# A cross-attention block with a recurrent mixer: set-up inside the score buffers, first loads in order of need, exponentials and late loads held at set places

## The chip, the cores and the metric

The kernel runs on one core of a Trainium2 chip. Its engines are TensorE (PE: matrix products and transposes), VectorE (DVE), ScalarE (ACT), GpSimd (POOL) and the sync engine (SP), which here issues the DMA transfers. Each engine works through its own list of instructions in order. The metric is the time of one execution on the device in microseconds (us); the median of the runs is compared. All numbers are float32.

## The reference

Three layers follow one another on x, 32 batches of 64 rows of 256:

```python
x = x + xattn(layernorm(x), ctx_768, w_q, w_kv, w_out, b_out)
x = x + attn(layernorm(x), time_decay, time_first, time_mix_*, Wk, Wv, Wr, Wo, bo)
x = x + ffn(layernorm(x), w1, b1, w2, b2)
```

The first is cross-attention with 16 heads of 64 over 1601 context rows of 192 per batch: q from x, k and v from the context, softmax over the keys, a projection back to 256. The second mixes each row with the one before it, makes k, v and r with Wk, Wv, Wr, runs a decaying sum over the 64 rows (decay exp(-exp(time_decay))), divides, gates by a sigmoid and projects with Wo. The third is two matrix products with a relu between them.

## The kernel before, in words

Keys are never formed. The key weights are folded into the queries instead: for each head, q times the transposed key weights gives a vector of 192 that is multiplied with the context rows themselves. The 192 are held as 128 ("lo") and 64 ("hi").

**Set-up.** The key half of w_kv (`wk_lo`, `wk_hi`) is transposed by TensorE into `wkT` (L304, L305, evicted at L308). Then `queries(tg)` runs for four groups `tg` of eight batches (512 rows of x). It normalises four tiles of x (statistics L110, L111, `xn` L177), transposes them (`xnT`, L185, L188), and for four head groups `g` of four heads each makes q (`q_ps`, L195, evicted as `qT` by ScalarE, L202), the folded lo part (`ql_ps`, L211, evicted as `q_lo` half by VectorE L218 and half by ScalarE L219) and the hi part (`qh_ps`, L226, evicted as `q_hi` by VectorE, L233, L234). Each head group is stored to a DRAM tensor `q_dram` (L236, L242). `q_lo` and `q_hi` have two buffers each, so the group after next waits for the store to have landed. PSUM holds six banks for the folded parts and two for all else. `q_load(b)` brings one batch's folded queries back (L163). `blocks_load(b)` loads the context of a batch in blocks of 32 columns (`cb`, twelve transfers, L153), and `ctx_prep(b)` turns these on VectorE into the transposed context `cT` (stream transposes L260, L261), with two small transfers (L255, L262).

**Late weights.** The weights wanted only later (`wv_lo`, `wv_hi`, `wo_sb`, the four square matrices `nat_*`, biases and per-channel columns) are loaded in set-up, after the first block loads, on the sync queue. At the end of set-up TensorE transposes the square matrices into `rw_T` (L320, evicted by VectorE L325); `td_rows`, rows of the decay, are made from two exponentials (L328 to L331).

**Attention.** The main loop goes over 64 half-batches `u`: a batch `b` and eight of its heads. `scores` makes for 1601 keys the products of `cT` and q: six blocks of twelve products of 512 columns (L475) and a rest (L494). ScalarE copies each block from PSUM to `s_sb` (L482, L501); there are two PSUM buffers for blocks and two buffers of `s_sb`. VectorE keeps a running maximum `m2` (L484, L486), then `mx` (L504, L505); GpSimd reduces it over partitions into `mb` (L512). Four parts follow, each a subtraction on VectorE (L522) and an exponential on ScalarE (L523). While the scores of half `u` run, the previous half's exponentials are summed on VectorE (`t2`, `sum`, L547 to L551), reduced by GpSimd (`den`, L555) and inverted (L565 to L569); its weighted sums `o_lo` (L344, called from `av_lo`) and `o_hi` (L592, L602) come after the scores, and VectorE scales them into `oT` (L618). The loop is a software pipeline: at `u == 1` the parts of half 0 are given to `scores` as hooks, called after blocks 2, 3, 4 and 5; later halves do their parts after `av_lo`. `fill` places pieces of the older tiles' work (projections, mixer) between the products of `av_lo`. The feed-forward layer closes the program.

**What sets the order.** A planner orders each engine's list at build time, by the program's order, priorities and modelled readiness; it may move an instruction forward where it thinks the operands are ready. On the chip each list is then fixed. A tile of a pool shares memory with earlier tiles that were released: set-up's pool is closed before the pool `attn` (scores, maxima) opens, so the first uses of `attn` wait for the last readers and transfers of what lay there.

Of the kernel before, what the change touches and what calls it, by code (L numbers as in the profile page):

```python
# [15 lines left out]
P = 128  # L16
# [4 lines left out]
def kernel(  # L21
# [69 lines left out]
    nc.sync.dma_start(x_sb[:, 0:4, :], xr[:, 0:4, :])  # L91
# [25 lines left out]
    with ExitStack() as st_b:  # L117
        with ExitStack() as st_a:
            kp = st_a.enter_context(tc.tile_pool(name="keys", bufs=2))
            cpool = st_a.enter_context(tc.tile_pool(name="ctx", bufs=1))  # L120
            aw = st_a.enter_context(tc.tile_pool(name="aw", bufs=1))
            wv_lo = aw.tile([P, INNER], F32, name="wv_lo")
            wv_hi = aw.tile([P, INNER], F32, name="wv_hi")
            wo_sb = aw.tile([P, INNER // P, D], F32, name="wo_sb")
# [44 lines left out]
            def queries(tg, sp, sps, wq_sb, wkT):  # L169

                TG = QB * T
                NX = TG // P
# [8 lines left out]
                xnT = sp.tile([P, 2, TG], F32, tag="xnT", name=f"xnT_{tg}")  # L181
                for c in range(2):
# [5 lines left out]
                    nc.vector.tensor_copy(xnT[:, c, :], pt)  # L188
                for g in range(NP // 2):
                    qT = sp.tile([P, 2, TG], F32, tag="qT", name=f"qT_{tg}_{g}", bufs=6)  # L190
                    for k in range(2):
                        hp = 2 * g + k
                        pq = sps.tile([P, TG], F32, tag="ps", name=f"q_ps_{tg}_{hp}")
                        for c in range(2):
                            nc.tensor.matmul(  # L195
                                pq,
                                lhsT=wq_sb[:, c, hp * P : (hp + 1) * P],
                                rhs=xnT[:, c, :],
                                start=(c == 0),
                                stop=(c == 1),  # L200
                            )
                        nc.scalar.activation(qT[:, k, :], pq, AF.Copy, scale=HD**-0.5)  # L202
                    lo = sp.tile([P, QB, 4, T], F32, tag="q_lo", name=f"q_lo_{tg}_{g}", bufs=2)
                    hi = sp.tile([P, QB, 2, T], F32, tag="q_hi", name=f"q_hi_{tg}_{g}", bufs=2)
                    for k in range(2):
                        pl = [
                            sps.tile([P, QB, T], F32, tag="f", name=f"ql_ps_{tg}_{g}_{k}_{o}", bufs=6)
                            for o in range(2)
                        ]
                        for o in range(2):  # L210
# [648 lines left out]
```

## Time and profile before

| | us |
|---|---|
| median of 3 runs | 2618.55 (2616.88 to 2618.9) |
| the profiled execution's own time | 2618.07 |
| its span | 2616.2 |
| TensorE busy in the span | 2588.2 |
| VectorE busy | 1908.3 |
| ScalarE busy | 953.6 |
| GpSimd busy | 356.4 |
| DMA, share of 16 engines (main queue) | 33.1% |

A profile row gives a start or a total, a duration, the engine and line, what is written and read, sizes and count; in brackets stands how long the engine was idle before it and what released it. A matrix product of float32 is shown as two instructions. Products are pipelined and their ends are modelled, so a busy TensorE may still be slowed by what it waits for. The granted clock of TensorE is 1.00 at full speed; the mean over this execution is 0.997.

### The profile page before, as it was taken

The page shows a single profiled execution, that of the slowest core. Times are in us where ns is not written, and L with a number is a line of the kernel's source. Part 1 is how long each engine was busy: PE and PEld are TensorE (multiplying, and loading weights), DVE is VectorE, ACT ScalarE, POOL GpSimd, SP SyncE. Part 2 cuts the span into 40 slices and gives each one's busy share as a digit, 9 for nine tenths or more (in the row PEclk, how much of TensorE's full clock was granted, in tenths as well). Part 3 has the DMA queues.
Part 4 walks back from the last instruction along what each step waited for, and adds up shares of the span by engine and source line. Part 5 has one row for each costly group of instructions (what it writes and reads, how often), then busy time and mean ns, then how long its engine had stood idle before and what let it go on. Part 6 is the DMA issues. An engine that isn't in the chain of part 4 may idle for free.

```text
span 2616.2 us, 33242 instructions
## 1 busy us (share of the span) xinstructions
PE 2588.2 (99%) x13824; PEld 1129.4 (43%) x13824; DVE 1908.3 (73%) x2283; ACT 953.6 (36%) x1019; POOL 356.4 (14%) x176
## 2 busy tenths in 40 slices
PE   8989999999999999999999999999999999999999
PEld 3333344444444444444444444444344444444466
DVE  4468878777786878777787868777787868787741
ACT  2233334333333334343433333343433434343221
POOL 0001111111111111111111111111111111111100
PEclk9989999999999999999999999999999999999999
DMA  8983333333322323233331323333331323310100
GB/s 201 273 174 54 58 56 63 45 63 63 63 57 50 60 42 63 45 63 63 63 63 44 63 39 63 49 59 63 63 63 44 63 49 54 63 26 20 52 11 22
DMA packets 437799, 169.63 MB, mean 65 GB/s; under 512 B 332400, under 2 KB 423952, under 8 KB 437648
## 3 DMA queue, kind: packets, MB, share of 16 engines
q1 hardware_dynamic: 437104, 166.46, 33.1%
q8 instruction: 108, 1.77, 0.3%
q10 hardware_dynamic: 544, 1.05, 0.1%
q14 instruction: 43, 0.35, 0.1%
HBM read 138.60 MB, written 27.26 MB: 63 GB/s over the span
## 4 chain that ended last, share of the span: by engine, by line
PE 95%; DMA 2%; DVE 1%; SPq 1%; issue 0%; POOL 0%; ACT 0%; DVEq 0%; POOLq 0%; ACTq 0%
PE s_ps L475 38%; PE o_lo L344 28%; PE o_hi L592 13%; PE s_ps_r L494 3%; PE fy L784 2%; PE v_ps L638 2%; PE h_ps L770 2%; PE y_ps L344 2%; PE q_ps L195 1%; DMA q_dram<-q_lo 1%; PE o_hi L602 1%; PE Wk_ps L344 1%; PE Wr_ps L344 1%; PE Wv_ps L344 1%; PE ry L344 1%; SPq L242 0%
## 5 line engine op out<-in xcount | busy, mean ns | idle before, releaser
L475 PE MATMUL s_ps<-q,cT 64*128 64x512 f32 x4608 | 1010.3, 594 | 8.0 <-ACT s_sb L482 7.1
L344 PE MATMUL o_lo<-s_sb,c 128*64 128x512 f32 (+1 forms) x3328 | 741.6, 594 | 0.0
L482 ACT COPY s_sb<-s_ps 128x1024 f32<-128x1024 f32 x384 | 388.7, 1012 | 955.6 <-PE s_ps L475 944.2
L475 PEld LDWEIGHTS s_ps<-q,cT 64*128 64x128 f32 x4608 | 442.2, 188 | 547.6 <-issue 537.9
L523 ACT ACTIVATE s_sb<-s_sb 128x2048 f32<-128x2048 f32 (+1 forms) x256 | 398.7, 1586 | 460.7 <-DVE s_sb L522 460.7
L522 DVE TENSOR_TENSOR s_sb<-s_sb,mb 128x2048 f32<-128x2048 f32 (+1 forms) x256 | 470.4, 1886 | 101.9 <-POOL mb L512 101.9
L486 DVE TENSOR_TENSOR m<-m,s_sb 128x1024 f32<-128x1024 f32 x256 | 313.6, 1225 | 169.6 <-ACT s_sb L482 157.7
L344 PEld LDWEIGHTS o_lo<-s_sb,c 128*64 128x64 f32 (+1 forms) x3328 | 231.1, 137 | 427.4 <-issue 417.7
L592 PE MATMUL o_hi<-s_sb,c 128*64 128x512 f32 x1536 | 340.4, 592 | 0.0
L555 POOL PARTITION_ALL_REDUCE den<-sum x64 | 207.4, 3241 | 834.1 <-DVE oT L618 666.3
L549 DVE TENSOR_TENSOR t<-t,s_sb 128x1024 f32<-128x1024 f32 x256 | 310.7, 1214 | 4.4
L512 POOL PARTITION_ALL_REDUCE mb<-mx x64 | 114.2, 1785 | 897.7 <-DVE mx L505 897.7
L565 DVE STREAM_TRANSPOSE turned<-den 128x512 f32<-128x512 f32 x64 | 45.5, 711 | 222.1 <-POOL den L555 222.1
L592 PEld LDWEIGHTS o_hi<-s_sb,c 128*64 128x64 f32 x1536 | 109.3, 136 | 211.3 <-issue 206.1
L494 PE MATMUL s_ps_r<-q,cT 64*65 64x256 f32 x768 | 93.5, 376 | 0.0
L260 DVE STREAM_TRANSPOSE cT<-cb 128x768 f32<-128x768 f32 x96 | 92.7, 967 | 0.0
L484 DVE TENSOR_TENSOR m<-s_sb 128x1024 f32<-128x1024 f32 x64 | 75.7, 1183 | 9.0 <-DMA cb<-in_ctx_dram 8.5
L547 DVE TENSOR_TENSOR t<-s_sb 128x1024 f32<-128x1024 f32 x64 | 77.7, 1214 | 0.0
L494 PEld LDWEIGHTS s_ps_r<-q,cT 64*65 64x65 f32 x768 | 54.0, 134 | 52.8 <-issue 33.5
L102 POOL TENSOR_TENSOR rstd_ln<-rstd_ln,root 128x1 f32<-128x1 f32 (+1 forms) x24 | 32.3, 1347 | 278.6 <-DVE rstd_ln L101 278.6
L195 PE MATMUL q_ps<-xnT,wq_sb 128*128 128x512 f32 x128 | 62.2, 626 | 0.0
L344 PE MATMUL y_ps<-wo_sb,outT 128*64 128x256 f32 x512 | 58.0, 379 | 0.0
(111 smaller groups left out, 1491.0 us busy)
## 6 DMA issues: line engine op xcount, KB each, us to landing
q<-q_dram SPq DMA_DIRECT2D x64, 768.0 KB, 6.7
c<-in_ctx_dram SPq DMA_DIRECT2D x32, 1152.0 KB, 6.2
cb<-in_ctx_dram SPq DMA_DIRECT2D x192, 104.0 KB, 4.3
cb<-in_ctx_dram SPq DMA_DIRECT2D x192, 96.0 KB, 3.2
q_dram<-q_lo SPq DMA_DIRECT2D x16, 1024.0 KB, 8.8
q_dram<-q_hi SPq DMA_DIRECT2D x32, 256.0 KB, 6.7
x_sb<-in_x_dram SPq DMA_DIRECT2D x4, 512.0 KB, 8.8
w_sb<-in_L_ffn_w_dram SPq DMA_DIRECT2D x2, 1024.0 KB, 5.1
```

What stands on the lines that cost most here:

```text
L260: nc.vector.transpose(cT[:, s, 0 : NB1 * BL], c[:, s, 0:NB1, :])
L344: nc.tensor.matmul(out[rs], lhsT=lhsT[:, rs], rhs=rhs, start=start, stop=stop, skip_group_check=True,)
L475: nc.tensor.matmul(ps[:, k, :], lhsT=cT[rs, s, i * P : (i + 1) * P], rhs=q[rs, s, js : js + HALF], start=(s == 0), stop=(s == NS - 1),)
L482: nc.scalar.copy(s_sb[:, 2 * i : 2 * i + 2, :], ps)
L486: nc.vector.tensor_tensor(m2, m2, s_sb[:, 2 * i : 2 * i + 2, :], ALU.max)
L494: nc.tensor.matmul(ps[0:KR, k, 0:HH], lhsT=cT[rs, s, NB1 * BL : KT + 1], rhs=q[rs, s, js + k * HH : js + (k + 1) * HH], start=(s == 0), st ...
L512: nc.gpsimd.partition_all_reduce(mb, mx, P, bass_isa.ReduceOp.max)
L522: nc.vector.tensor_tensor(s, s, m, ALU.subtract)
L523: nc.scalar.activation(s, s, AF.Exp)
L549: nc.vector.tensor_tensor(t2, t2, p[:, 2 * i : 2 * i + 2, :], ALU.add)
L555: nc.gpsimd.partition_all_reduce(self.den, self.sum, P, bass_isa.ReduceOp.add)
L592: nc.tensor.matmul(self.ph[o * C2 : (o + 1) * C2, :], lhsT=self.ctx[:, self.at[c], P:C], rhs=self.s_sb[:, c, :], start=(c < 2), stop=False ...
```

## The change

The diff below is cut to its core. In words:

- `wk_lo`, `wk_hi`, `wq_sb`, `wkT` and the six `qT` slots are now parts of two tiles `room` of the score buffers' tag `s_sb`, in the pool `attn`, which opens before set-up. The sums, the inverse, `oT`, `outT` and the late weights move to a pool `late`, opened after set-up's pool has closed.
- All first loads go on the sync queue in the order wk (first half), x (two pieces), wk (second half), wq (two halves), more x, blocks. ScalarE issues none.
- `wkT` is evicted by ScalarE.
- `queries` works on pairs `e` of head groups: four q products of pairs of heads, then both folded lo parts, then the hi parts of the pair, with one `q_hi` tile and two hi stores of four heads each. The next group's rows are normalised and transposed within the current one (`normed_x`, `turned_x`), and `xnT` has two buffers. In the last pair, half of the hi evictions are ScalarE's.
- The late weights are loaded by `late_loads`, called at `u == 0` behind the last store of set-up; the square matrices come in eight pieces into buffers of the mixer's pool.
- The transposes of the square matrices (`turn`) move into `av_lo` of half 1 (run at `u == 2`, after its products 2, 5, 8 and 11), with evictions by ScalarE; the decay's steps (`decay`) move to `u == 3`.
- At `u == 1` the parts of half 0 are called after blocks 3, 4 and 5; hooks and fills are queued behind the copy or product at which they stand (`issue_after`: order on that engine only). `blocks_load`, `q_load` and `late_loads` of the first batches are queued behind the last store; `ctx_prep(1)` behind the maximum of half 1.

```diff
-    nc.sync.dma_start(x_sb[:, 0:4, :], xr[:, 0:4, :])
...
-                for g in range(NP // 2):
-                    qT = sp.tile([P, 2, TG], F32, tag="qT", name=f"qT_{tg}_{g}", bufs=6)
+            def queries(tg, xnT, copied, sp, sps, wq_sb, wkT, room):
+                more = tg + 1 < B // QB
+                following = None, None
+                for e in range(NP // 4):
+                    if e == 0 and more:
+                        with tc.issue_after(copied.ins):
+                            xn = normed_x(tg + 1, sp)
+                    hi = sp.tile([P, QB, 4, T], F32, tag="q_hi", name=f"q_hi_{tg}_{e}", bufs=2)
...
+                    for g in (2 * e, 2 * e + 1):
+                        slot = (tg * NP // 2 + g) % 6
+                        qT = room[1][:, slot * 2 * TG : (slot + 1) * 2 * TG].rearrange(
+                            "p (k t) -> p k t", k=2
+                        )
...
+                    if e == 1 and more:
+                        following = turned_x(tg + 1, xn, sp, sps)
...
+                        if e == 1 and not more:
+                            nc.scalar.copy(hi[:, :, 2 * k + 1, :], ph[1])
+                        else:
+                            nc.vector.tensor_copy(hi[:, :, 2 * k + 1, :], ph[1])
...
+                room = [
+                    ap.tile([P, NCK * HALF], F32, tag="s_sb", name=f"room_{k}", bufs=2)
+                    for k in range(2)
+                ]
...
-                    nc.scalar.dma_start(wq_sb[:, :, ns], wqr[:, :, ns])
+                halves = [slice(n * INNER // 2, (n + 1) * INNER // 2) for n in range(2)]
+                for n, ns in enumerate(halves):
                     nc.sync.dma_start(wk_lo[:, ns], w_kv[0:P, ns])
                     nc.sync.dma_start(wk_hi[:, ns], w_kv[P:C, ns])
+                    if n == 0:
+                        nc.sync.dma_start(x_sb[:, 0:2, :], xr[:, 0:2, :])
+                        nc.sync.dma_start(x_sb[:, 2:4, :], xr[:, 2:4, :])
+                for ns in halves:
+                    nc.sync.dma_start(wq_sb[:, :, ns], wqr[:, :, ns])
...
+                    nc.scalar.copy(wkT[:, 2 * g : 2 * g + 2, :], ps)
...
+            nats = {}
+            aw = st_a.enter_context(tc.tile_pool(name="late", bufs=1))
...
+            def late_loads():
                 nc.sync.dma_start(wv_lo, w_kv[0:P, INNER : 2 * INNER])
...
+            def turn(n):
+                ps = bank([P, 2, D], f"rw_ps_{n}")
+                for hc in range(2):
+                    for oc in range(2):
+                        nc.tensor.transpose(
+                            ps[:, hc, oc * P : (oc + 1) * P],
+                            nats[n][oc][:, hc * P : (hc + 1) * P],
+                            ident,
+                        )
+                nc.scalar.copy(rw_T[n], ps)
...
-                    for hook in hooks.get(i, ()):
-                        hook()
+                    with tc.issue_after(copied.ins):
+                        for hook in hooks.get(i, ()):
+                            hook()
...
-                        for work in fill.get(c, ()):
-                            work()
+                        with tc.issue_after(done.ins):
+                            for work in fill.get(c, ()):
+                                work()
...
-                if phase == 1 and i >= 0:
+                if u == 2:
+                    fill = {c: [lambda n=n: turn(n)] for c, n in zip((2, 5, 8, 11), nats)}
+                elif u == 3:
+                    fill = {6: [lambda: decay(top)]}
+                elif phase == 1 and i >= 0:
...
-                    hooks = {i + 2: [part] for i, part in enumerate(parts)}
+                    hooks = {3: parts[0:1], 4: parts[1:2], 5: parts[2:]}
...
+                if u == 1:
+                    with tc.issue_after(top.ins):
+                        cT_next = ctx_prep(1)
...
+                if u == 0:
+                    with tc.issue_after(store.ins):
+                        late_loads()
```

## Prediction

> **What bounds the kernel now.** I read the page first, for the engines and the chain that ended last.
>
> ```profile
> span 2616.2 us, 33242 instructions
> PE 2588.2 (99%) x13824; PEld 1129.4 (43%) x13824; DVE 1908.3 (73%) x2283; ACT 953.6 (36%) x1019; POOL 356.4 (14%) x176
> PE 95%; DMA 2%; DVE 1%; SPq 1%; issue 0%; POOL 0%; ACT 0%; DVEq 0%; POOLq 0%; ACTq 0%
> ```
>
> TensorE is the bound: 28.0 us of the span are idle, and the chain leaves TensorE for 5%. In order of time, all that lies before 205 us; from there the chain is nothing but TensorE (72 score matmuls in 15.65 us, 52 of o_lo in 11.31, again and again). The order of the instructions from the fourth half-batch on is the same in both programs, so the change can act only on the first 205 us. There the timeline of TensorE comes second.
>
> ```profile
> 7.83 0.45 PE L304 MATMUL wkT_ps<-ident,wk_lo 128*128 128x128 f32 x1 [7.83 <-DMA wk_lo<-in_L_xattn_w_kv_dram]
> ...
> 14.21 1.97 PE L185 MATMUL xnT_ps<-ident,xn 128*128 128x128 f32 x8
> 16.11 5.79 PE L195 MATMUL q_ps<-xnT,wq_sb 128*128 128x512 f32 x8
> ...
> 24.77 3.70 PE L195 MATMUL q_ps<-xnT,wq_sb 128*128 128x512 f32 x8
> ...
> 42.83 14.05 PE L195 MATMUL q_ps<-xnT,wq_sb 128*128 128x512 f32 x32
> ...
> 75.51 1.34 PE L226 MATMUL qh_ps<-qT,wkT 64*64 64x512 f32 x8
> ...
> 83.41 2.11 PE L211 MATMUL ql_ps<-qT,wkT 64*128 64x512 f32 x8
> 86.59 1.68 PE L226 MATMUL qh_ps<-qT,wkT 64*64 64x512 f32 x8 [1.07 <-DVE q_hi L233]
> ```
>
> The reader is to see that set-up begins 7.8 us late, that the first eight q_ps take 5.79 us against 3.70 later (half clock), and that groups stretch (qh_ps 1.09 us at its best, 1.68 here). What stretches them is a buffer: q_lo has two, and its evictions wait for the stores to DRAM (19.0 us of VectorE's waits and 34.2 of ScalarE's). The sync queue tells why the stores are late: ahead of the first lie the late weights.
>
> ```profile
> 21.36 0.84 SPq L281 DMA_DIRECT2D wv_lo<-in_L_xattn_w_kv_dram  x1
> ...
> 36.31 0.49 SPq L236 DMA_DIRECT2D q_dram<-q_lo  x1
> ```
>
> Third, the ramp into attention, all engines in order of time:
>
> ```profile
> 140.08 1.12 PE L320 MATMUL rw_ps_Wr<-ident,nat_Wr 128*128 128x128 f32 x4 [2.70 <-DVE Wk_T L325]
> ...
> 142.88 17.68 PE L475 MATMUL s_ps<-q,cT 64*128 64x512 f32 x72 [0.83 <-issue]
> ...
> 167.94 2.29 DVE L522 TENSOR_TENSOR s_sb<-s_sb,mb 128x2048 f32<-128x2048 f32 x1 [2.13 <-POOL mb L512]
> ...
> 175.76 0.99 ACT L482 COPY s_sb<-s_ps 128x1024 f32<-128x1024 f32 x1
> ...
> 176.80 9.95 PE L475 MATMUL s_ps<-q,cT 64*128 64x512 f32 x36 [7.13 <-ACT s_sb L482]
> ```
>
> The 7.13 us are the largest hole after the start: on ScalarE the second eviction of half 1 stands behind two exponentials of half 0, and these wait for VectorE's subtractions. And VectorE alone, then TensorE alone, later:
>
> ```profile
> 231.99 7.29 DVE L522 TENSOR_TENSOR s_sb<-s_sb,mb 128x2048 f32<-128x2048 f32 x4 [1.99 <-POOL mb L512]
> ```
> ```profile
> 238.72 15.72 PE L475 MATMUL s_ps<-q,cT 64*128 64x512 f32 x72
> ```
>
> From the subtractions of half 0 (167.94) to those of half 2 (231.99) VectorE needs 64.05 us; only some 11 of them are waits for GpSimd's reductions. That is the number on which my forecast hangs.
>
> **The change, part by part.** T0 is the first score matmul (142.88 before).
>
> First loads. The x rows and the two wq loads of ScalarE's queue no longer go ahead of wk. In the trace x, issued at 0.72, had landed at 6.31 with wq in the same 16 engines; the windows behind it moved about 300 GB/s. With some 1.0 us to the first packet and 0.5 us after the last, 384 KB of wk land at about 3.5 us, x (0.9 MB in all) at 5.2. The wkT transposes take 8 x 0.70 us, to 9.2; x needs 4.6 us from landing to xn (6.33 to 10.89 before), ready at 9.4. xnT 1.9 us: q_ps starts at 11.3, not 16.11. If the queue brings no more than before, the gain is nothing. The wkT evictions move from VectorE to ScalarE, idle until 19.9; without that cover, 2 us.
>
> Set-up work at full clock: q_ps 128 x 0.44 = 56.2; ql 16 x 1.92 = 30.7; qh 16 x 1.02 = 16.3; the other xnT 3 x 1.1 = 3.4; together about 107. Regrouping qh by eight heads changes no count on TensorE. The cold start costs 2.1 us before (5.79 - 3.70); I take 2.6, since where the clock's window falls is chance. The step to the scores 0.8 (142.88). Before, that makes 16.1 + 2.1 + 107 + 0.8 = 126.0, the rw turns 2.2, their wait 2.7 and their half clock 1.0: the remaining 11 us are waits for stores.
>
> Stores. The 17 issues of late weights (now 21) go from between the block loads and the first store to behind q of batch 1, so the first store leaves at some 24 us, not 36.3. One pair of head groups asks 3 MB of stores per 13 us of TensorE; before, the stores of a pair went out every 11 us when they were late (issues at 64.04, 74.36 and 85.45), so the queue keeps up. q_hi takes two issues per pair, not four. What is late next: in tg 0, the normalisation of the next rows and the first stream transposes (some 10 us of VectorE) stand ahead of the q_lo evictions, covered by only six q_ps products of tg 1 (5.3 us): about 2 us of stall there, 1 to 2 where tg 1 follows, 1 in tg 1, 1 around the load of q. Together 5, from 1 to 12 (as before).
>
> T0 = 11.3 + 2.6 + 107 + 0.8 + 5 = 126.7, 16.2 earlier.
>
> Ramp. Room for the scores now shares the buffers of wk, wq and qT, read last by TensorE, so the first eviction waits for no store (11.26 us on ScalarE before, hidden but for half clock). Four evictions of half 1 go ahead of the first exponential. By the durations of the trace: mb of half 0 at T0 + 21.5, eviction 3 done at T0 + 28.6, exponential at 30.5, eviction 4 at 31.5: the 7.13 us hole is gone, half 2's scores start at T0 + 50.8 (62.07 before). The stream transposes of batch 1 go behind the maximum of half 1; they wait for nothing there.
>
> But VectorE has as much to do as before. From the subtractions of half 0 at T0 + 21.5 to those of half 1 it has these four (7.3), five m (6.3), four t2 (4.9), mx (1.4) and the stream transposes (3.2): 23.1, so T0 + 44.6 (30.46 before). What was put off then comes: subtractions 7.2, t2 and sum 2.6, the wait for den 3.4, the inverse with t2 4.1, t2, two oT and sum 5.0, the second wait for den 3.4, inverse 1.7, five m with transposes and mx 10.9, reduction 2.0: 40.3, so half 2's are at T0 + 84.9. Together 63.4, where the trace has 64.05. TensorE however reaches the end of half 1 eleven us sooner.
>
> The turns of Wk, Wv, Wr, Wo (16 transposes, 4 x 0.55 us) now lie inside o_lo of half 1, and their evictions on ScalarE: Wk_T, an exponential of half 2, Wv_T, two exponentials, Wr_T. The two banks alternate, so the turn of Wo waits for the copy of Wv_T, that for the exponential, that for the first subtraction: T0 + 84.9 + 2.3 + 1.9 + 0.6 = T0 + 89.7. TensorE is there at T0 + 67.7 + 10.4 + 1.65 = T0 + 79.8. Queued behind are the last o_lo, all of o_hi, and half 3's scores. A stall of 10 us, which is new. The bounds: nothing if VectorE had no backlog; 13 if den is late as well.
>
> Then the clock. The windows of the trace for the 7.13 us hole:
>
> ```profile
> 174.00:175.00 1.00, 0.00 (x0) 0.00 (x0) 1.00 (x1) 1.00 (x1) 0.00 (x0) 0.50 0.95 151
> 177.00:180.00 3.00, 3.00 (x8) 1.32 (x10) 3.00 (x3) 2.97 (x3) 0.00 (x0) 0.50 1.54 140
> 181.00:182.00 1.00, 1.00 (x8) 0.51 (x6) 0.90 (x2) 0.35 (x1) 0.00 (x0) 1.00 1.60 125
> ```
>
> The granted clock was 0.50 from about 174 to 180.6, so 4 us of resumed work ran at half: 2.0 us. The Trainium skill (TensorE: Matmul & The Clock Gate, Part 1) has half clock after an idle window of some 3.4 us and full clock after one busy window: 1.7 us. By its Part 4, transposes don't count as busy; in the trace the drop at 139.8 came with a hole of only 2.70 us, with transposes ahead, and lasted to 146.6. As this stall ends in transposes too, I take that nearer case: 1.1 us of them and 5.1 of dense work at half, 3.1. By Part 1 alone the result would be 1.4 us lower.
>
> Half 3's scores start at T0 + 67.7 + 11.2 + 2.2 + 5.7 + 10 + 3.1 = T0 + 99.9 = 226.6, against 238.72: 12.1 us earlier. All after it is the same. Profiled execution: 2618.07 - 12.1 = 2606.0; the median is 0.5 above the profiled one: 2606.
>
> td's copy, exponentials and rows in half 3 (under 2 us of VectorE) and the late loads are covered: o_lo of half 1 needs the first 50 us after they are queued; cT's copy behind them is due at T0 + 66 and leaves at 45.
>
> **Rivals.** (1) The ramp goes as ordered and the turn of Wo finds its bank free: T0 + 86.8, 25 us earlier, 2593. For it: the planner put the turns there. Against it: 64.05 us of VectorE. (2) Set-up stays paced by stores (its waits 11 to 16, not 5, since q's load and c's now go in between): T0 133 to 138, 2612 to 2617. For it: 8.8 us to landing of a q_lo store; against it the 12 us of head start. (3) Slower: VectorE comes out of the ramp behind. Subtractions stood 6.73 us ahead of the next scores at 238.72, and some 5 are needed, or ScalarE evicts late. Should it stay below this, each of the 60 halves left pays; from 0.2 us a half the gain is gone, at 0.4 it is 2618.5 + 12 = 2630. Against it: the 13 us stall lets VectorE catch up, and the order from half 3 on is as before. (4) Nothing moves, because the head and the stores were hidden: 2618; the idle rows speak against it.
>
> **How the numbers follow.** The likeliest, 0.57: 2606, its own range 2598 to 2613. (1) 0.17; (2) 0.16, half of it within 0.2%; (3) 0.05; (4) 0.05. Measurement can tell about 0.2%, 5 us. Faster 0.80, same 0.14, slower 0.06. The range, 2591 to 2617, takes in (1) and (2).
>
> **What would show it.** Right: q_ps near 11, a first q_lo store before 26, the first score matmul between 122 and 132, no hole at half 1's third block, a hole of 7 to 12 us at rw_ps_Wo released by Wv_T, then 0.50 of clock. Wrong: rw_ps_Wo without idle time (rival 1), DMA waits on q_lo of 30 us or more (rival 2), or holes at s_ps after 240 us (rival 3).

## The result, and the profile after

| | before | after |
|---|---|---|
| median of 6 runs, us | 2618.73 (2616.88 to 2620.27) | 2603.58 (2601.7 to 2604.73) |
| span of the profiled execution, us | 2616.2 | 2603.0 |
| first score matmul, T0 | 142.88 | 125.99 |
| half 3's scores | 238.72 | 225.87 |

The changed kernel takes 0.9942 of the time before, with a 95% interval of 0.9929 to 0.9955: 15 us less, where some 12.5 had been forecast (2606). Five more runs of it, beside later experiments, gave 2603.42 (0.9946, 0.9932 to 0.9959).

The page of the changed kernel: the span, the engines' busy time, and the chain that ended last.

```profile
span 2603.0 us, 33212 instructions
PE 2581.6 (99%) x13824; PEld 1130.0 (43%) x13824; DVE 1903.2 (73%) x2274; ACT 959.5 (37%) x1029; POOL 357.2 (14%) x176
PE 95%; DMA 2%; DVE 1%; SPq 1%; POOL 0%; issue 0%; ACT 0%; DVEq 0%; POOLq 0%; ACTq 0%
```

TensorE idles 21.4 us, not 28.0, and is busy 6.6 us less for the same 13824 instructions (their clock and their waits count as busy). The timeline of TensorE tells where; each row gives start, duration, engine, line, what is made from what, and in brackets the idle time before it and what ended it. The count behind x is of instructions, two to a product.

```profile
4.14 0.45 PE L321 MATMUL wkT_ps<-ident,room 128*128 128x128 f32 x1 [4.14 <-DMA room<-in_L_xattn_w_kv_dram]
5.32 0.37 PE L322 MATMUL wkT_ps<-ident,room 64*128 64x64 f32 x1 [0.73 <-DMA room<-in_L_xattn_w_kv_dram]
...
8.59 0.45 PE L321 MATMUL wkT_ps<-ident,room 128*128 128x128 f32 x1 [0.80 <-DMA room<-in_L_xattn_w_kv_dram]
...
13.27 9.22 PE L213 MATMUL q_ps<-xnT,room 128*128 128x512 f32 x16
...
27.93 7.13 PE L213 MATMUL q_ps<-xnT,room 128*128 128x512 f32 x16
...
121.47 1.13 PE L231 MATMUL ql_ps<-room,room 64*128 64x512 f32 x4 [0.91 <-DVE q_lo L238]
...
125.99 15.72 PE L526 MATMUL s_ps<-q,cT 64*128 64x512 f32 x72 [0.84 <-ACT q_hi L261]
...
142.81 15.72 PE L526 MATMUL s_ps<-q,cT 64*128 64x512 f32 x72
...
176.66 15.72 PE L526 MATMUL s_ps<-q,cT 64*128 64x512 f32 x72
...
215.29 1.11 PE L385 MATMUL rw_ps_Wo<-ident,nat_Wo 128*128 128x128 f32 x4 [8.95 <-ACT Wv_T L390]
...
218.09 7.41 PE L647 MATMUL o_hi<-s_sb,c 128*64 128x512 f32 x24
...
225.87 15.72 PE L526 MATMUL s_ps<-q,cT 64*128 64x512 f32 x72
```

Set-up's waits are almost gone; half 1's scores (142.81) run without the 7.13 us hole; and the new hole stands where it was forecast, at the turn of Wo, released by the copy of Wv_T. The other two engines of that wait, VectorE's subtractions and ScalarE's part of the chain:

```profile
147.51 7.29 DVE L576 TENSOR_TENSOR s_sb<-s_sb,mb 128x2048 f32<-128x2048 f32 x4 [1.98 <-POOL mb L566]
...
169.90 7.29 DVE L576 TENSOR_TENSOR s_sb<-s_sb,mb 128x2048 f32<-128x2048 f32 x4
...
210.46 7.29 DVE L576 TENSOR_TENSOR s_sb<-s_sb,mb 128x2048 f32<-128x2048 f32 x4 [1.91 <-POOL mb L566]
```
```profile
212.85 1.91 ACT L577 ACTIVATE s_sb<-s_sb 128x2048 f32<-128x2048 f32 x1 [15.24 <-DVE s_sb L576]
214.67 0.57 ACT L390 COPY Wv_T<-rw_ps_Wv 128x512 f32<-128x512 f32 x1
```

Wv had been turned at 199.64, but ScalarE's list has an exponential of half 2 ahead of the copy, and that waits for the subtraction of 210.46. I call the start of half 2's subtractions S2; it is what the experiments below turn on. The windows of the same stretch (length, busy time of PE, PEld, DVE, ACT and POOL, then the granted clock, DMA share and GB/s) show what comes behind:

```profile
209.00:215.00 6.00, 0.00 (x0) 0.00 (x0) 4.54 (x3) 2.15 (x2) 1.43 (x1) 0.50 1.21 127
215.00:217.00 2.00, 1.71 (x6) 1.01 (x8) 2.00 (x1) 2.00 (x2) 0.00 (x0) 0.50 0.00 0
217.00:219.00 2.00, 2.00 (x8) 0.53 (x6) 1.90 (x4) 1.79 (x2) 0.00 (x0) 0.50 0.03 8
219.00:221.00 2.00, 2.00 (x8) 0.66 (x6) 1.97 (x2) 1.64 (x4) 0.00 (x0) 0.50 0.00 0
221.00:223.00 2.00, 2.00 (x8) 0.52 (x6) 1.90 (x3) 0.00 (x0) 0.00 (x0) 0.68 0.00 0
223.00:225.00 2.00, 2.00 (x12) 0.65 (x10) 1.97 (x3) 0.00 (x0) 0.00 (x0) 1.00 0.00 0
```

TensorE works from 215.29 on, and gets half its clock until about 222.3.

### The profile page after: what moved, and what is told of

Same layout as the page of the kernel before. It is cut to its first block, busy times and chain, and to the rows that moved or that the text cites. A ratio compares the mean times of both kernels' runs of the same rounds, so it can differ in the third digit from the quotient of the medians.

```text
span 2603.0 us, 33212 instructions
## 1 busy us (share of the span) xinstructions
PE 2581.6 (99%) x13824; PEld 1130.0 (43%) x13824; DVE 1903.2 (73%) x2274; ACT 959.5 (37%) x1029; POOL 357.2 (14%) x176
## 4 chain that ended last, share of the span: by engine, by line
PE 95%; DMA 2%; DVE 1%; SPq 1%; POOL 0%; issue 0%; ACT 0%; DVEq 0%; POOLq 0%; ACTq 0%
PE s_ps L526 37%; PE o_lo L371 27%; PE o_hi L647 13%; PE s_ps_r L546 3%; PE fy L850 2%; PE v_ps L693 2%; PE q_ps L213 2%; PE h_ps L836 2%; PE y_ps L371 2%; PE ql_ps L231 1%; PE o_hi L657 1%; SPq L149 1%; PE qh_ps L252 1%; PE Wr_ps L371 1%; PE Wk_ps L371 1%; PE Wv_ps L371 1%
## 5 line engine op out<-in xcount | busy, mean ns | idle before, releaser
L213 PE MATMUL q_ps<-xnT,room 128*128 128x512 f32 x128 | 59.4, 617 | 0.0
```

The source lines that it names most:

```text
L213: nc.tensor.matmul(pq, lhsT=wq_sb[:, c, hp * P : (hp + 1) * P], rhs=xnT[:, c, :], start=(c == 0), stop=(c == 1),)
```

## The experiments

Medians are compared within one set of runs, each with its own runs of the kernel before (medians 2616.63 to 2617.85); ratios are to those.

### The changed kernel again

> The changed kernel once more, unedited, as the measure for the runs beside it: 2603.6 within 2 us. What it can show besides: whether the first q_ps group (9.22 us against 7.13 at full clock) and the products behind the wait at rw_ps_Wo (o_hi 7.41 against 5.32) differ between two executions of one program. If the clock's windows run free of the program, the first group lies anywhere between 7.4 and 9.3 us; if the clock follows the work, it is 9.22 again within 0.1.

2603.42 us. The first group of q_ps in this run:

```profile
12.93 8.51 PE L213 MATMUL q_ps<-xnT,room 128*128 128x512 f32 x16
```

One program, two executions: this group took 8.51 us here and 9.22 above, o_hi behind the wait at Wo 7.13 and 7.41. The profiles' rows give 1.00 as granted clock at the start, but the clock record of a trace begins only with its first entry, which is full clock at 15.7 us here and at 17.5 above. With half clock until then, half of the time from the group's start is lost: 1.4 us here and 2.1 above, which is what the group took beyond its later 7.13. Around Wo the wait (8.95 and 8.97), the turn and the last o_lo agree to 0.02 us; only o_hi differs, since half clock went on for 6.5 us behind the restart in this run and for 7.0 above. So the clock changes at times that the instructions alone don't fix.

T0 moves with it: 124.76 here, 125.99 above; 0.7 of these 1.2 us are clock, the rest an earlier start and shorter waits. A microsecond at T0 between two runs therefore means nothing, and S2 is better read from T0 (84.49 and 84.47).

### Two turns in half 2, two in half 3

```diff
-                if u == 2:
-                    fill = {c: [lambda n=n: turn(n)] for c, n in zip((2, 5, 8, 11), nats)}
-                elif u == 3:
-                    fill = {6: [lambda: decay(top)]}
+                if u in (2, 3):
+                    two = list(nats)[2 * (u - 2) : 2 * (u - 1)]
+                    fill = {c: [lambda n=n: turn(n)] for c, n in zip((2, 5), two)}
+                    if u == 3:
+                        fill[6] = [lambda: decay(top)]
```

> The changed kernel with its four turns spread: Wk and Wv behind products 2 and 5 of half 2's pass (which multiplies half 1), Wr and Wo behind products 2 and 5 of half 3's pass. Half 2 then asks for no bank that stands behind its own exponential. Theory A (VectorE's backlog sets the pace, the bank only shows it): the 8.95 us wait at rw_ps_Wo goes, and with it the half clock behind it (3.5 us), but half 3's third score block waits some 4 us, because its bank is emptied by a ScalarE copy that stands behind half 2's exponential: 9 to 10 us faster than the changed kernel, about 2594. Theory B (the loss lies in the bank alone): all 12.5 us come back, about 2591. Theory C (TensorE only gets to wait elsewhere for the same VectorE work): the wait at half 3's scores is 9 us or more, and the time stays at 2601 to 2604.

2596.57 us (0.9920, 0.9906 to 0.9933), 7 us faster than the changed kernel. TensorE's timeline of this run:

```profile
210.50 5.42 PE L526 MATMUL s_ps<-q,cT 64*128 64x512 f32 x24
219.18 12.27 PE L526 MATMUL s_ps<-q,cT 64*128 64x512 f32 x48 [3.25 <-ACT s_sb L533]
```

The wait at the turn is gone and a shorter one stands at half 3's third score block. So the loss lay neither in the bank alone (theory B: all comes back) nor is it handed on whole (theory C). Theory A has the shape right and 2 to 3 us too much gain: it left out the clock. The 48 instructions behind 3.25 us of idling take 12.27 us where they take 10.57 at full clock: 1.70 lost.

### The second context prepared ahead of half 0's scores

```diff
+                    if tg == 2:
+                        b_tiles[1] = blocks_load(1)
...
-                if u == 1:
-                    with tc.issue_after(top.ins):
-                        cT_next = ctx_prep(1)
...
+            cT_next = ctx_prep(1)
             c_tiles = {}
```

> The changed kernel with the block transposes of the second context (four VectorE transposes, about 3.3 us) taken out of half 1: its blocks are loaded behind the stores of the third group of queries, and it is prepared ahead of half 0's scores, where VectorE is idle for 6.6 us. The turns stay where they are. Theory A (VectorE's backlog): the subtractions of halves 1 and 2 come about 3.3 us earlier, the wait at rw_ps_Wo shrinks from 8.95 to about 5.6 us, and the time by 3 to 4 us, to about 2600. Theory B (the bank and ScalarE's own work set the wait): the wait at rw_ps_Wo stays within 1 us of 8.95 and the time within 1.5 us of 2603.6. A third possibility: the loads meet the last stores of the queries and T0 comes later by 1 us or more, which would show in the first score matmul.

2605.14 us (0.9955, 0.9942 to 0.9967): nothing gained. TensorE, then VectorE:

```profile
122.17 1.30 PE L231 MATMUL ql_ps<-room,room 64*128 64x512 f32 x4 [3.39 <-ACT q_lo L239]
...
215.01 1.11 PE L387 MATMUL rw_ps_Wo<-ident,nat_Wo 128*128 128x128 f32 x4 [6.88 <-ACT Wv_T L392]
```
```profile
171.48 7.29 DVE L578 TENSOR_TENSOR s_sb<-s_sb,mb 128x2048 f32<-128x2048 f32 x4 [1.68 <-POOL mb L568]
...
210.19 7.29 DVE L578 TENSOR_TENSOR s_sb<-s_sb,mb 128x2048 f32<-128x2048 f32 x4 [1.91 <-POOL mb L568]
```

With T0 at 127.79, S2 came at T0 + 82.40 instead of T0 + 84.47: 2.07 us earlier, and the wait at the turn shrank by exactly that, from 8.95 to 6.88. Theory A's link holds one to one; its size (3.3) does not, because with less work of its own VectorE now waits 1.68 us for GpSimd's maximum at half 1. The third possibility came true too. TensorE waited 3.39 us at the end of set-up for an eviction of q_lo on ScalarE, which stood 4.9 us behind a store, and half clock for 3.4 us followed (1.8 us more). T0 is only 1.8 us later than in the changed kernel because the cold start was 1.7 us cheaper in this execution (q_ps x16 in 7.55 us). Gain and loss cancel.

### Both

> Both edits: the turns spread over halves 2 and 3, and the second context prepared ahead of half 0's scores. Theory A: no wait at rw_ps_Wo, and that of half 3's third score block goes from about 4 to about 1 us: some 13 us faster than the changed kernel, about 2590 to 2592. If the bank alone had been the cause (theory B), this run gives nothing beyond the run with spread turns (within 1.5 us of it).

2595.76 us (0.9917, 0.9903 to 0.9930), 1 us below spread turns alone, not 2590 to 2592. TensorE's timeline:

```profile
220.64 10.57 PE L528 MATMUL s_ps<-q,cT 64*128 64x512 f32 x48 [1.17 <-ACT s_sb L535]
```

In the ramp it goes as theory A has it: the wait at the third block falls from 3.25 to 1.17 us, and behind so short a wait no clock is lost. But T0 is 128.07, 3.5 us later than with spread turns alone, and takes nearly all of it back: set-up ends, as in the run before, with a wait of 3.31 us and 3.4 us of half clock.

### Three more maxima on VectorE

```diff
+                if u == 1:
+                    for k in range(3):
+                        nc.vector.tensor_tensor(
+                            m2, m2, s_sb[:, 2 * k : 2 * k + 2, :], ALU.max
+                        )
                 nc.vector.tensor_tensor(mx, m2[:, 0, :], m2[:, 1, :], ALU.max)
```

> The changed kernel with three more running maxima on VectorE (128 x 1024 each, 1.22 us, the same data once more) ahead of half 1's mx: 3.7 us of work more in the backlog, nothing else. Theory A: the subtractions of halves 1 and 2 come 3.7 us later, the wait at rw_ps_Wo grows from 8.95 to 12.6 us and the time by 3.7 us, to about 2607.3. Theory B (the bank and ScalarE's own work set the wait): the wait stays within 1 us of 8.95 and the time within 1.5 us of the unedited kernel.

2604.11 us (0.9946, 0.9934 to 0.9959), which is the changed kernel's time: by the number, theory B. The timelines of TensorE and of VectorE say something else.

```profile
187.46 12.37 PE L526 MATMUL s_ps<-q,cT 64*128 64x512 f32 x48 [5.60 <-ACT s_sb L533]
...
216.80 0.66 PE L385 MATMUL rw_ps_Wo<-ident,nat_Wo 128*128 128x128 f32 x4 [3.00 <-ACT Wv_T L390]
...
218.29 7.02 PE L652 MATMUL o_hi<-s_sb,c 128*64 128x512 f32 x24
```
```profile
177.29 7.29 DVE L581 TENSOR_TENSOR s_sb<-s_sb,mb 128x2048 f32<-128x2048 f32 x4 [1.88 <-POOL mb L571]
...
211.98 7.29 DVE L581 TENSOR_TENSOR s_sb<-s_sb,mb 128x2048 f32<-128x2048 f32 x4 [1.99 <-POOL mb L571]
```

And a row of VectorE in the changed kernel, where it waits for GpSimd's sum `den`:

```profile
184.05 0.71 DVE L619 STREAM_TRANSPOSE turned<-den 128x512 f32<-128x512 f32 x1 [3.13 <-POOL den L609]
```

Half 1's subtractions came 7.6 us later (T0 + 51.51, not T0 + 43.91), so half 2's third score block now waits 5.60 us; the wait at the turn then is only 3.00. TensorE waits in two places for the one backlog. The "nothing else" of the expectation did not hold. Of the 7.6 us 3.5 are the maxima and 1.88 a new wait for GpSimd's maximum; the rest is work on the sums, which the planner moved ahead of these subtractions and which therefore no longer comes behind them. So S2 came only 1.73 us later, not 3.7: the 3.13 us of waiting for `den` are gone, the 1.88 have come. And these 1.73 us were paid back by the clock: behind 8.95 us of idling the restart lost 3.4 us, behind 3.00 only 1.70 (o_hi 7.02 against 5.32); the block behind 5.60 us lost another 1.80.

So far the runs give one account. TensorE's release follows S2 by a fixed distance, set by ScalarE's list:

| run | T0 | S2 - T0 | where TensorE waits last | release - S2 |
|---|---|---|---|---|
| changed kernel | 125.99 | 84.47 | turn of Wo, 8.95 | 4.83 |
| early context | 127.79 | 82.40 | turn of Wo, 6.88 | 4.82 |
| more maxima | 125.78 | 86.20 | turn of Wo, 3.00 | 4.82 |
| spread turns | 124.53 | 84.48 | third block, 3.25 | 10.17 |
| both | 128.07 | 82.40 | third block, 1.17 | 10.17 |
| ramp alone (below) | 141.28 | 87.56 | third block, 4.88 | 10.17 |

Released at the turn, TensorE still has the rest of o_lo, o_hi and two score blocks ahead of the third block, which in the changed kernel starts at S2 + 20.7; with the turns spread it starts at S2 + 10.17. Six more runs, above and below, keep the two distances to 0.01 us: 4.82 in those with the turn of Wo in half 2, 10.16 or 10.17 in those with spread turns.

### The ramp's part alone

The kernel before with these lines of the change (and `top` returned by `scores`):

```diff
-                    hooks = {i + 2: [part] for i, part in enumerate(parts)}
+                    hooks = {3: parts[0:1], 4: parts[1:2], 5: parts[2:]}
...
+                    with tc.issue_after(copied.ins):
+                        for hook in hooks.get(i, ()):
+                            hook()
...
+                if u == 1:
+                    with tc.issue_after(top.ins):
+                        cT_next = ctx_prep(1)
```

> The kernel before with the ramp's part alone: the parts of half 0 as hooks behind blocks 3, 4 and 5 of half 1's scores, hooks queued behind the copy at which they stand, the second context's preparation behind the maximum of half 1. Set-up, its turns, its loads and its stores stay as before, so the first score matmul stays near 142.9. Theory A (VectorE's backlog): the 7.13 us hole and its half clock go, but half 3's third score block waits 3 to 4 us as in the run with spread turns: half 3's scores in effect at T0 + 89.8 instead of T0 + 95.8, 6 us faster than before. Rival 1 (the hole was the whole loss): 9 us faster. Rival 2 (TensorE gets to wait elsewhere for all of it): within 2 us of before.

2616.05 us (0.9993, 0.9986 to 0.9999): 1.8 us, where theory A said 6. Rival 2 holds. Rows of TensorE, then of VectorE:

```profile
194.86 15.72 PE L475 MATMUL s_ps<-q,cT 64*128 64x512 f32 x72
...
239.01 12.93 PE L475 MATMUL s_ps<-q,cT 64*128 64x512 f32 x48 [4.88 <-ACT s_sb L482]
```
```profile
228.84 7.29 DVE L525 TENSOR_TENSOR s_sb<-s_sb,mb 128x2048 f32<-128x2048 f32 x4 [1.91 <-POOL mb L515]
```

The 7.13 us hole is gone (half 2's scores at T0 + 53.6, not T0 + 62.0), and 4.88 us of waiting and 2.4 us of half clock stand at half 3's third block. The hole was never a loss of its own. Before, that block started at 238.72 + 5.30 = 244.0, or S2 + 12.0, against the 10.17 at which it can: TensorE came 1.9 us after its release, and no more than that could be had there without S2 moving. S2 did move a little here, to 228.84, half of it by an earlier T0 (141.28); these 3.15 us and the 1.9 came in, and the 2.4 us of half clock went out again. What moved the end in the changed kernel is S2 itself: 231.99 to 210.46.

### The old first loads

```diff
+                nc.sync.dma_start(x_sb[:, 0:4, :], xr[:, 0:4, :])
+                for n in range(2):
+                    ns = slice(n * INNER // 2, (n + 1) * INNER // 2)
+                    nc.scalar.dma_start(wq_sb[:, :, ns], wqr[:, :, ns])
                     nc.sync.dma_start(wk_lo[:, ns], w_kv[0:P, ns])
```

> The changed kernel with the old first loads: rows of x first on SyncE's queue, the query weights on ScalarE's queue, key weights between. By my account of the set-up, the first q_ps then starts near 16.1 instead of 13.27, nothing after it changes, and the first score matmul comes 2.8 us later, near 128.8: about 2606.4. Rival: the delay is taken up by waits later in the set-up (2.8 us of them are left), and the time stays within 1 us of 2603.6.

2606.28 us (0.9958, 0.9946 to 0.9971), as expected to 0.1 us, though not in detail. TensorE's timeline, then a row of VectorE:

```profile
15.93 9.23 PE L213 MATMUL q_ps<-xnT,room 128*128 128x512 f32 x16
...
46.82 1.45 PE L231 MATMUL ql_ps<-room,room 64*128 64x512 f32 x2 [1.27 <-DVE q_lo L238]
48.20 3.26 PE L252 MATMUL qh_ps<-room,room 64*64 64x512 f32 x16
...
222.30 6.66 PE L644 MATMUL o_hi<-s_sb,c 128*64 128x512 f32 x24
```
```profile
46.09 2.48 DVE L238 COPY q_lo<-ql_ps 128x512 f32<-128x512 f32 x4
```

q_ps starts 2.66 us later, yet T0 is 130.18, 4.2 us later. A new wait of 1.27 us comes on top: VectorE was normalising the next rows and transposing context until 46.09 and emptied a bank late. The prediction had set about 2 us of waiting for this place; in the changed kernel it costs nothing. Half clock for 3.4 us followed (qh_ps x16 3.26 us, not 1.95), 1.6 us lost; two waits of the changed kernel, 1.35 us, are gone. The restart behind the turn was 0.75 us cheaper. The profiled execution is the slowest of the five (2608.13), so the agreement to 0.1 us is in part luck. The first loads are worth some 3 us.

### The late weights, from both sides

The changed kernel with the square matrices and the bias rows (1.4 MB) back behind the first block loads:

```diff
                 b_tiles = {0: blocks_load(0)}
+                nats = {}
+                tags = iter(("xn", "in_k", "in_v", "in_r", "e", "ev", "num", "den"))
+                for n, w in (("Wk", Wk), ("Wv", Wv), ("Wr", Wr), ("Wo", Wo)):
...
+                    nc.sync.dma_start(bias_rows[:, n, :], v.partition_broadcast(P))
```

> The changed kernel with 1.4 MB of the late weights (the square matrices and the bias rows) back ahead of the first store. By my prediction's account the first store leaves some 5 us later, and the first score matmul comes 3 to 5 us later than 124.8 to 126.0: 2607 to 2608.5. Rival (the DMA engines have a pause from 35 to 45 us, share 0.20, that takes the delay up; what counts is traffic after 50 us): first score matmul within 1 us of 126, time 2602.5 to 2604.5. The wait at rw_ps_Wo stays near 8.95 in both.

2606.40 us (0.9963, 0.9949 to 0.9977): 3 us slower, between the two expectations. The first q_lo store left at 28.45 (25.2 in the changed kernel), T0 was 128.45. TensorE's timeline has the place:

```profile
68.97 2.07 PE L231 MATMUL ql_ps<-room,room 64*128 64x512 f32 x2 [1.80 <-DVE q_lo L238]
...
217.75 1.12 PE L385 MATMUL rw_ps_Wo<-ident,nat_Wo 128*128 128x128 f32 x4 [8.96 <-ACT Wv_T L390]
```

The 1.80 us are a wait for VectorE, which again was normalising the next rows (until 68.2), and 6.8 us of half clock behind it cost 3.3 more; 5.1 us together. T0 moved by only 2.5 to 3.7 because, among other things, the cold start was cheaper (q_ps x16 in 7.74 us). How the later stores bring VectorE's lateness about stays open. The pause of the DMA engines from 35 to 45 us was used (their share rose from 0.20 to 0.54 there) and did not take up the whole delay. The other side, the kernel before with wv, wo and the bias rows behind the last store:

```diff
-                nc.sync.dma_start(wv_lo, w_kv[0:P, INNER : 2 * INNER])
...
+                with tc.issue_after(store.ins):
+                    nc.sync.dma_start(wv_lo, w_kv[0:P, INNER : 2 * INNER])
...
                 for n, nat in nats.items():
```

> The kernel before with one part of the change: the late weights that set-up itself doesn't need (wv, wo and the bias rows, 2.4 of 3.4 MB) queued behind the last store; the square matrices, columns and turns stay in set-up. My prediction's account (the late loads ahead of the first store are what makes the stores late, 11 us of waits): the first q_lo store leaves some 8 us earlier than 36.3, VectorE's and ScalarE's waits on q_lo shrink, and the first score matmul comes 5 to 8 us earlier than 142.9, the time 4 to 8 us below before. Rival: in the trace of before the DMA engines are two thirds idle from 45 to 65 us (share 0.32 and 0.37) because TensorE then runs 32 q products in a row, which give nothing to store, and full from 65 on; a head start is lost in that pause, and the waits come from the bunched order. Then the first score matmul moves by 2 us at most and the time by 2 at most.

T0 came 5.2 us earlier, at 137.69, and the waits for q_lo stores on VectorE and ScalarE fell from 53.3 to 19.5 us, as my account had it; the time hardly moved, as the rival had it (2614.82, 0.9991, 0.9983 to 0.9999). TensorE's timeline:

```profile
137.69 15.76 PE L479 MATMUL s_ps<-q,cT 64*128 64x512 f32 x72 [0.83 <-issue]
...
169.17 13.21 PE L479 MATMUL s_ps<-q,cT 64*128 64x512 f32 x48 [9.18 <-ACT s_sb L486]
```

The hole at half 1 grew to 9.18 us with 2.6 us of half clock. The planner also set the second context's transposes ahead of half 0's subtractions, and they waited 4.25 us for blocks that are now queued with the late weights; the subtractions came at T0 + 26.23 and S2 at T0 + 89.27. In the profiled execution 4.4 us of the 5.2 are left at half 3's scores; the medians show 1.8, and this kernel's runs spread over 5 us (2611.76 to 2616.93). How much of it the moved loads are worth there stays open.

### Where the second context's blocks may go

Three runs look for a place for early blocks that costs set-up nothing; all have the turns spread. First the twelve block loads on GpSimd's queue (`blocks_load(1, nc.gpsimd)`):

> The run with both edits (spread turns, second context prepared early), but with the twelve block loads of the second context on GpSimd's queue instead of between the stores on SyncE's. There they had put the q_lo store behind them 8 us later (115.99 instead of 107.91) and TensorE had waited 3.3 us for it. If that queue order was the cause of the later first score matmul, it comes back from 128.1 to between 124.5 and 126.2, and the time falls by 2 to 3.5 us below the run with both edits, to about 2592 to 2593. If the loads cost by their traffic (the DMA engines shared with the stores) or by VectorE's transposes standing ahead of the q_lo copies, T0 stays at 127.5 to 128.5 and the time within 1 us of 2595.8.

2599.70 us (0.9932, 0.9920 to 0.9945): neither of the two expectations, but 3 to 4 us slower than on SyncE's queue. GpSimd had nothing ahead of them and issued all twelve between 44 and 55 us; the timeline shows what they met:

```profile
58.68 1.70 PE L252 MATMUL qh_ps<-room,room 64*64 64x512 f32 x8 [4.67 <-ACT q_lo L239]
60.31 8.29 PE L213 MATMUL q_ps<-xnT,room 128*128 128x512 f32 x16
```

T0 was 131.65. In the changed kernel the DMA engines' share is 0.86 to 1.01 in eight of ten windows of 10 us from 25 on (below it only at 35 to 55), so a load there meets the stores. Here it met one on which an eviction waited 5.9 us, and TensorE with it; half clock behind that wait took 1.8 us more. Then the loads at their place on SyncE's queue, with the context rows of batch 0 (1.2 MB, as much) taken out of set-up; the second context's transposes, not shown in the cut, move behind VectorE's last eviction of q_hi:

```diff
                 if j == 0:
-                    c_tiles[b] = ctx_load(b)
+                    with tc.issue_after(store.ins):
+                        c_tiles[b] = ctx_load(b)
```

> The run with both edits (spread turns, second context early), with as much traffic taken out of set-up as was put in: the context rows of batch 0 (1.2 MB, wanted only by half 0's weighted sums) go behind the last store, the block loads of the second context keep their place, and its transposes stand behind the last q_hi eviction on VectorE, where it is idle. If the 3.3 us that set-up lost were the price of 1.2 MB at the 280 GB/s at which the DMA engines are full (4.3 us), the first score matmul comes back from 128.1 to between 124.5 and 126.2, and the time to 2592 to 2593.5. If they were the price of the queue (twelve issues that put the q_lo store 8 us later), it stays at 127.5 to 128.5 and the time within 1 us of 2595.8.

2595.92 us (0.9924, 0.9912 to 0.9937), the same as without the swap; T0 127.28, with 3.15 and 0.68 us of waiting at the end of set-up. So neither the bytes nor transposes ahead of the q_lo copies were the cause. No half clock followed the 3.15 us. The sync queue's rows show why equal bytes are not equal:

```profile
103.68 12.63 SPq L149 DMA_DIRECT2D cb<-in_ctx_dram  x12
116.42 2.06 SPq L241 DMA_DIRECT2D q_dram<-q_lo  x2
```

The twelve block loads (rows of 32 numbers) hold the queue for 12.6 us; the context rows, in the changed kernel, for 2.5. What counts is which store stands behind. The last run puts the blocks behind the q_hi stores of the last group's first pair, ahead only of stores for which nothing in set-up waits, and the transposes behind a maximum of half 0; as in the run before, the context rows of batch 0 go behind the last store:

```diff
+                    if e == 0 and not more:
+                        with tc.issue_after(store.ins):
+                            b_tiles[1] = blocks_load(1)
...
+                    if u == 0 and i == 3:
+                        with tc.issue_after(high.ins):
+                            early.append(ctx_prep(1))
```

> The changed kernel with spread turns, and the second context prepared early at a place that no store of set-up stands behind: its twelve block loads go behind the q_hi stores of the last group's first pair (ahead of the last pair's stores, for which nothing in set-up waits), its four transposes behind the third running maximum of half 0, where VectorE has gaps of 1.35 us, and the context rows of batch 0 behind the last store. If the place in the queue was the whole price of the early keys, the first score matmul stays at 123.5 to 125 (as with spread turns alone, or up to 1 us earlier), half 3's third block waits about 1.2 us and not 3.25, and the time falls 2.5 to 4.5 us below the run with spread turns: 2592 to 2594. If VectorE's transposes at this place push half 0's maximum back instead (the blocks land later than T0 + 13), half 0's subtractions come later than T0 + 21.5 by as much and the gain is gone: 2595 to 2597.

2591.33 us (2590.72 to 2591.95; 0.9901, 0.9884 to 0.9917), the fastest of all and a little below the 2592 to 2594 expected: 12 us below the changed kernel. TensorE's timeline:

```profile
122.66 15.72 PE L529 MATMUL s_ps<-q,cT 64*128 64x512 f32 x72 [0.84 <-ACT q_hi L261]
...
215.80 10.57 PE L529 MATMUL s_ps<-q,cT 64*128 64x512 f32 x48 [1.74 <-ACT s_sb L536]
```

No wait is shown between the first q_ps and T0 but the 0.84 of the hand-over; S2 at 205.64, T0 + 82.98, since the four transposes delayed half 0's subtractions by 0.45 us; the third block at S2 + 10.16; no clock lost behind it. Against spread turns alone these are 5.2 us: 1.9 by an earlier T0, 1.5 by the shorter wait at the third block and 1.7 by the half clock that did not follow it. T0 is earlier because two short waits at the end of set-up are gone and the cold start was cheaper; whether the place of the blocks or that of the context rows removed them was not tested apart.

## Why the prediction was right, by its own steps

**First loads.** q_ps at 11.3; measured 13.27. This step was 2 us off: wk landed 0.6 us later than my rate gave, and its pieces did not land together (0.73 us for the hi rows, 0.80 for the second half; both are in the rows above). I had set one landing time for all of it. Undone, the step costs about 3 us.

**Cold start.** 2.6; measured 2.1, and 0.4 to 2.1 over all runs with this set-up. Chance, as said.

**Set-up work.** 107. From 125.99, less the start, 2.09 of cold clock, 0.91 + 0.44 of waits and the 0.84 of the hand-over, 108.4 are left.

**Stores.** 5 us of waits; measured 1.35. The range given, 1 to 12, just holds it. VectorE and ScalarE wait for q_lo stores 8.8 us in all, not 53.3, and 19.9 in the second execution, with TensorE waiting 1.35 and 1.17 us: I booked evictions that wait as TensorE that waits, but there are six banks between. The four errors, +2.0, -0.5, +1.4 and -3.65, leave T0 0.7 us from the forecast of 126.7: the sum was better than its terms. Of the 16.9 us by which T0 came earlier, the first loads gave some 3, the late weights 2.5 to 5 (by the two runs, which differ), and 5.9 were the turns with their wait and their half clock. What is left may come from the pairs of head groups and from preparing the next rows earlier; neither was tested apart.

**Ramp.** Half 2's scores T0 + 50.8; measured T0 + 50.67. Subtractions at T0 + 21.5, 44.6 and 84.9; measured 21.52, 43.91 and 84.47. The number on which the forecast hung, 63.4 us of VectorE, was 62.95, and it decided: rival 1 (2593, the bank found free) failed on it. Rival 2 (set-up stays paced by stores) failed on the 1.35 us; rival 3 had no sign, no hole stands at a score block after 240 us.

**The turn of Wo.** Arrival T0 + 79.8, release T0 + 89.7, stall 10; measured 80.3, 89.3 and 8.95. The order of the events, Wv_T behind the exponential behind the subtraction, was right to the instruction.

**Clock.** 3.1 us by the nearer case. Measured, from the excess of the turn, the last o_lo and o_hi over their full-clock times: 0.45 + 0.90 + 2.09 = 3.4, and 2.3 to 3.5 in the four other runs that wait 6.9 to 9.0 us there. Where dense products resumed, behind 3.25 to 9.18 us of idling, it was 1.7 to 2.6. The reason given for the nearer case, that transposes don't count as busy (the Trainium skill, TensorE: Matmul & The Clock Gate, Part 4), is not shown by any run: four transposes and dense work stand behind each of these waits at the turn, and the two ranges overlap. In the clock records of these traces, the start and the end of the program aside, half clock comes in stretches of 3.4, 6.8, 10.2 or 13.7 us, so what a restart loses hangs on where the last stretch ends. That 3.1 was forecast and 3.4 came is partly luck.

**The end.** Half 3's scores at T0 + 99.9 = 226.6; measured T0 + 99.88 = 225.87. The profiled execution of the changed kernel took 2604.73, 1.3 us under the forecast, 0.7 of it by T0. The other half of the 2.4 us between forecast and median is the choice of the execution: the profiled one is the slowest of its six, where the forecast put the median above it.

What the prediction did not see though it had the numbers: in its own sum the ramp loses 4 us against before (T0 + 99.9 against T0 + 95.84). It told the removal of the 7.13 us hole as a gain of 11 and the stall as a new loss. Both are one thing, VectorE's backlog, as the run with the ramp alone showed. The gain of the change is that VectorE's ramp starts 16.9 us earlier with T0, 3.5 us earlier after T0 (half 0's subtractions at T0 + 21.52, not T0 + 25.06), and is 1.1 us shorter: 21.5 us at S2. Of these 12.85 arrived at half 3's scores; the other 8.7 were lost around the turn of Wo, because the turns stand in the half that runs ahead of VectorE. The run with spread turns got 7 us of that back.

## What to carry to other kernels

Before closing a hole on the bounding engine, look how long after its release the engine arrives at the next place where it depends on the engine behind (here 1.9 us, at half 3's third block). Of a longer hole only that much can be gained; the rest of the wait moves there, unless the engine behind gets done earlier. Measure from the event that releases (here half 2's subtractions), not from the hole: a fixed distance from it showed in these runs which edits could gain. And in this kernel a load was early only if no store that someone waits for stood behind it; its bytes said less than its place and the time it held the queue.

## What the runs showed of the hardware

- The first dense products lost 0.4 to 2.1 us to the cold clock, differently from execution to execution of one program too (q_ps x16: 7.55 to 9.22 us in ten executions, against 7.13 later). Full clock was first granted at 14.0 to 17.5 us.
- The length of a wait alone did not decide what it cost in clock. In set-up and among score products waits of 1.17, 1.74 and 3.15 us cost none, but 1.27 us cost 1.6, 1.80 us cost 3.3, 3.00 and 3.25 us cost 1.70, 4.88 us cost 2.4, and 6.9 to 9.0 us ahead of the turn 2.3 to 3.5. An idle window of some 3.4 us, after which the Trainium skill (TensorE: Matmul & The Clock Gate, Part 1) has half clock, was not needed: all four of these shorter waits that cost clock had half clock behind them. In the run with more maxima a shorter wait at the turn saved 1.7 us of clock, which is why 1.7 us of delay at S2 cost nothing there.
- Twelve block loads of 1.2 MB held the sync queue for 12.1 to 15.0 us in set-up, and for 7.8 later, at 260 us of the changed kernel; one load of 1.15 MB held it for 2.5 in set-up and for 0.4 later.
- The kernel before spreads over 5.8 us in all its runs (2614.45 to 2620.27), the changed one over 3 (2601.7 to 2604.73), and the last variant over 1.2 in four. No run here tells why.
